# Two attention layers on one core: the first weights, the first input piece and the first theta in another order

## The chip, the cores and the metric

The kernel runs on 1 core of a Trainium2 chip. The metric is the device time of one execution in microseconds, the median of several runs. Time before: 2462.61 us (three runs, 2462.26 to 2463.37).

## What is computed

Two non-local attention blocks, one after the other, on x of 4 x 128 x 96 x 96 (float32), each with its own weights:

```python
g_x = maxpool2(conv1x1(x, g_w, g_b))          # 64 channels, 2304 keys
theta_x = conv1x1(x, theta_w, theta_b)        # 64 channels, 9216 queries
phi_x = maxpool2(conv1x1(x, phi_w, phi_b))
f = einsum('bqc,bck->bqk', theta_x, phi_x)
y = einsum('bqk,bkc->bqc', softmax(f), g_x)
W_y = conv1x1(y, W_w, W_b)
inv = bn_gamma * rsqrt(bn_var + 1e-5)
out = W_y * inv + (bn_beta - bn_mean * inv) + x
```

## The kernel before, in words

The eight blocks (four images, two layers) are worked off in one long sequence of cycles. In a cycle TensorE makes scores of 128 keys against 1024 queries (`Pair.scores`, L707), ScalarE takes their exponential (L712), VectorE adds up the denominators (L721), and TensorE multiplies by the values (`Pair.values`, L729). Keys, values and queries of the next block are made in between. All engines run their instructions in the order in which the program is written.

The change lies in the first 20 us, in which the first block is prepared:

- **Loads.** `ws[0].load_gphi` (L170, issues at L173) brings g_w by ScalarE's queue and phi_w by SyncE's. `load_x(0, 12)` (L137, issues at L135) brings the first image by SyncE in twelve pieces of 768 pixels (eight image rows, 384 KB). `load_theta` (L177) brings theta_w by ScalarE, and `columns` (L267, issues at L274) three rows of parameters (theta's bias, two variances) by ScalarE too. Every landing counts up one of eight counters that are used in turn, so a later transfer waits until the counter's last transfer has landed.
- **Warm-up.** `busy` (L993) makes TensorE multiply the identity: five times before the transpose of the weights, three times behind it (`WARM`, L58).
- **Weights.** g_w and phi_w lie in one tile; TensorE turns it (L149) and VectorE copies it to `gphiT` (L151). theta_w is turned by VectorE in eight small transposes (`steps_theta`, L160).
- **Chunks.** The product of g and phi with x is made in chunks of 512 pixels (`products`, L352), pooled by VectorE (`pool`, L336) into `stage`. Chunk 0 and 1 are eight rows by 64 pixels, chunk 2 is the sixteen rows beside them by 32 pixels, chunk 3 begins in the third piece of x. `pooled_first` (L374) makes the first four: chunk 0, the upper half of chunk 2, chunk 1, the lower half of chunk 2, chunk 3. Chunks 2 and 3 share one PSUM tile. Behind `pooled_first`, VectorE centres the keys (`centring`, L407 and L408), and pools chunks 2 and 3.
- **First theta.** The first queries (`Pair.theta`, L671) follow as soon as chunks 2 and 3 are pooled in program order, in a PSUM tile of the pool that the odd pairs of chunks use as well. ScalarE takes them with the bias (`take_theta`, L701), behind the square roots of the variances (`make_std`, L187), the load of the table for exponentials (L1029) and a batch of keys (`batch`, L413 and L419). The parameter columns that both need are turned by VectorE (`first_cols`, L160 on `square_rows`).

PSUM tiles of the two pools concerned are reused in turn: chunks 6 and 7 write the buffer of chunks 2 and 3, chunks 10 and 11 that of theta, and so wait for its readers.

Of the kernel before, what the change touches and what calls it, by code (L numbers as in the profile page):

```python
# [9 lines left out]
F32 = mybir.dt.float32  # L10
# [6 lines left out]
P = 128  # L17
# [3 lines left out]
QT = 512  # L21
# [11 lines left out]
PT = 2 * QT  # L33
# [21 lines left out]
PREPARE = (1, 4, 10)  # L55
SQ = 32
EXPS = 5
WARM = (5, 3)  # L58
CYCLE = 2 * NB
ORDER = ((0, 0), (1, 0), (0, 1), (2, 0), (1, 1), (3, 0), (2, 1), (3, 1))  # L60
SHIFT = 35.0
# [4 lines left out]
def shifted_blocks(ctx: ExitStack, tc: tile.TileContext, x: bass.AP, layers, out: bass.AP, flag):  # L66
# [24 lines left out]
    nc = tc.nc  # L91
# [9 lines left out]
    ps_sc = ctx.enter_context(tc.tile_pool(name="ps_sc", bufs=2, space=PSUM))  # L101
# [28 lines left out]
    def new_x(b):  # L130
        return xp.tile([C, HW], F32, tag="x", name=f"x_{b}")

    def load_part(b, xt, i, n):
        src = x[b].rearrange("c h w -> c (h w)")
        nc.sync.dma_start(out=xt[:, ts(i, HW // n)], in_=src[:, ts(i, HW // n)])  # L135

    def load_x(b, n=6):  # L137
        xt = new_x(b)
        for i in range(n):
            load_part(b, xt, i, n)  # L140
        return xt

    def as_row(src):
        return src.rearrange("(o c) -> o c", o=1)
# [9 lines left out]
    def turned(dst, src):  # L154

        squares = [(i, j) for i in range(src.shape[0] // SQ) for j in range(src.shape[1] // SQ)]

        def step(some):
            for i, j in some:
                nc.vector.transpose(dst[ts(j, SQ), ts(i, SQ)], src[ts(i, SQ), ts(j, SQ)])  # L160

        return [lambda n=n: step(squares[n : n + 4]) for n in range(0, len(squares), 4)]
# [104 lines left out]
    def columns(wanted, name, engine, rows=None):  # L267

        if rows is None:
            rows = prep.tile([SQ, C], F32, name=f"rows_{name}")  # L270
        nc.vector.memset(rows, 0.0)
        for i, (w, key) in enumerate(wanted):
            n = w.p[key].shape[0]
            engine.dma_start(  # L274
                out=rows[i : i + 1, :].rearrange("o (h n) -> o h n", n=n),
                in_=as_row(w.p[key]).unsqueeze(1).to_broadcast([1, C // n, n]),
            )

        def make():
            cols = const.tile([C, SQ], F32, name=f"cols_{name}")  # L280
            for step in turned(cols, rows):
                step()
            for i, (w, key) in enumerate(wanted):
                w.col[key] = cols[:, i : i + 1]

        return make
# [15 lines left out]
    class Block:  # L302
# [68 lines left out]
                for i in range(2):  # L371
                    step(j * KB + i, pss[i])

        def pooled_first(self):  # L374

            pss = self.banks(0) + self.banks(1)
            self.products(0, pss[0])
            self.products(2, pss[2], lower=False)
            self.pool(0, pss[0])
            self.products(1, pss[1])  # L380
            self.pool(1, pss[1])
            self.products(2, pss[2], upper=False)
            self.products(3, pss[3])
            return pss[2:]

# [268 lines left out]
    class Pair:  # L654
# [14 lines left out]
        def theta(self, ps):  # L669
            for h in range(2):  # L670
                nc.tensor.matmul(  # L671
                    ps[ts(h, CI), :], lhsT=self.blk.w.theta,
                    rhs=self.runs(self.blk.xt)[:, h, :], start=True, stop=True,
                )
# [269 lines left out]
    def thetas(both):  # L944
# [13 lines left out]
        return crosswise(part, take)  # L958

    ws = [Layer(l, p) for l, p in enumerate(layers)]  # L960
    ws[0].load_gphi((nc.scalar, nc.sync))
    xs = {0: load_x(0, 12)}
    ws[0].load_theta(nc.scalar)
    first_cols = columns(
        [(ws[0], "theta_b"), (ws[0], "bn_var"), (ws[1], "bn_var")], "first", nc.scalar,
        square_rows,
    )
    nc.scalar.preload_act_table(AF.Sqrt)
# [18 lines left out]
    pairs = [Pair(blk, p, n * NP + p) for n, blk in enumerate(blocks) for p in range(NP)]  # L987
# [5 lines left out]
    def busy(n):  # L993
        for i in range(n):
            nc.tensor.matmul(warm[:, :P], lhsT=ident, rhs=ident, start=True, stop=True)
# [5 lines left out]
    b0 = blocks[0]  # L1001
    busy(WARM[0])
    ws[0].make_gphi()
    for step in ws[0].steps_theta():
        step()
    busy(WARM[1])
    second_batch = b0.pooled_first()
    b0.centring(KB)
    b0.batch(0)
    for j in range(1, FIRST):  # L1010
        if j == 1:
            for i in range(KB):
                b0.pool(KB + i, second_batch[i])
            first_cols()
        else:
            b0.pooled(j)
        if j == 1:
            th = ps_sc.tile([P, PT], F32, tag="sc", name="theta_ps_0")[:, :QT]
            pairs[0].theta(th)
        if j == 3:  # L1020
            pairs[0].take_theta(th)
        if j < FIRST - 2:
            b0.batch(j)
        for i, k in {2: [(0, 0)], 3: [(0, 1)], 4: [(0, 2)], 5: [(0, 3)], 6: [(1, 0), (1, 1)]}.get(j, []):
            b0.square(i, k)
        if j == 1:
            for w in ws:
                w.make_std()
            nc.scalar.preload_act_table(AF.Exp)  # L1029
    xs[1] = load_x(1)  # L1030


# [28 lines left out]
    for n in range(1, len(blocks)):  # L1061
        first = (n - 1) * NP * NB // CYCLE * CYCLE
# [21 lines left out]
    for t in range(total + 1):  # L1084
        q, s = 2 * (t // CYCLE), t % CYCLE
        even, odd = pairs[q : q + 2] if t < total else (None, None)
        first, second, take = None, *pending
        pending = (None, None)
        if t == 1:
            first = lambda: pairs[0].values(0)  # L1090
        unit, stage_of = stages.get(t, (None, None))
        assert unit is None or (t not in keys and second is None)
        if t in keys:
            n, i = keys[t]
            first, *pending = blocks[n].chunks(i)
        elif unit:
            first, take = unit.steps[stage_of]
# [11 lines left out]
        if t < total:  # L1109
            now, j = divmod(t, NB)  # L1110
# [11 lines left out]
            if t in loads:  # L1122
                b, i = loads[t]
# [19 lines left out]
        if t:  # L1143
            before, j = divmod(t - 1, NB)
# [312 lines left out]
def nonlocal_blocks(tc: tile.TileContext, x: bass.AP, layers, out: bass.AP):  # L1457
    with tc.tile_pool(name="flag", bufs=1) as pool:
        flag = pool.tile([1, 1], I32, name="flag")
        shifted_blocks(tc, x, layers, out, flag)  # L1460
        bad = tc.nc.values_load(flag[0:1, 0:1])
        with tc.If(bad > 0):
            general_blocks(tc, x, layers, out)
# [30 lines left out]
```

## Time and profile before

| | |
|---|---|
| median of 3 runs | 2462.61 us |
| profiled execution, its own time | 2461.85 us |
| span of the profiled execution | 2460.0 us |
| granted TensorE clock, mean | 1.00 |
| TensorE matmul busy | 2452.0 us, 100% |
| VectorE busy | 2068.4 us, 84% |
| ScalarE busy | 1645.3 us, 67% |
| GpSimd busy | 755.6 us, 31% |

The span is what the profiler saw of the program; the execution's own time holds 1.85 us more. In the profile PE is TensorE's matrix product, PEld its load of weights, DVE VectorE, ACT ScalarE, POOL GpSimd and SP SyncE; ACTq and SPq are these engines' issues of DMAs. Every float32 product of 512 columns shows as two records. A row of the timeline gives start and length in us, engine, line, what is written from what, and in brackets the idle time of the engine before it and what ended that.

### The profile page before, as it was taken

To read this page: it belongs to the slowest core of one execution; us is meant where nothing else is said; L and a number is where in the kernel's file an instruction comes from. 1 tells how busy PE (TensorE), PEld (TensorE's weight loads), DVE (VectorE), ACT (ScalarE), POOL (GpSimd) and SP (SyncE) were. 2 spreads that over 40 slices of the span, in tenths; PEclk is the share of its full clock that TensorE was granted. 3 is DMA by queue.
4 is the path that set the end of the run, shared out by engine and by line. 5 is a ranking of instruction groups with operands and counts; after the bars stand their busy time and mean duration, and the time that the engine had idled before them with its cause. 6 is when DMAs were issued, how large, how long until landed. Compare 5 with 4: busy or idle time off the path is not lost.

```text
span 2460.0 us, 58074 instructions
## 1 busy us (share of the span) xinstructions
PE 2452.0 (100%) x23325; PEld 903.0 (37%) x23325; DVE 2068.4 (84%) x2652; ACT 1645.3 (67%) x1789; POOL 755.6 (31%) x850
## 2 busy tenths in 40 slices
PE   9999999999999999999999999999999999999999
PEld 3333333333333333333333333333333333333333
DVE  8988888888788888888878888888887888877777
ACT  6666666666666666666666666666666666666665
POOL 1333333332233333333223333333322333322121
PEclk9999999999999999999999999999999999999999
DMA  6566676664467666776556676666645666643443
GB/s 190 97 105 123 126 143 115 114 120 88 89 112 133 125 128 127 139 142 136 104 94 122 122 135 121 127 124 112 120 83 100 118 133 123 122 89 82 82 87 65
DMA packets 188885, 283.85 MB, mean 115 GB/s; under 512 B 33334, under 2 KB 113344, under 8 KB 188608
## 3 DMA queue, kind: packets, MB, share of 16 engines
q0 software_dynamic: 91136, 137.68, 40.1%
q1 hardware_dynamic: 97304, 142.31, 20.0%
q8 instruction: 185, 3.03, 0.5%
q14 instruction: 92, 0.75, 0.1%
q10 hardware_dynamic: 168, 0.07, 0.0%
HBM read 54.07 MB, written 35.68 MB: 36 GB/s over the span
## 4 chain that ended last, share of the span: by engine, by line
PE 100%; DMA 0%; DVE 0%; SPq 0%; issue 0%; DVEq 0%
PE av L729 45%; PE sc L707 45%; PE unit_ps L495 5%; PE W_ps L874 2%; PE gphi_ps L352 1%; PE unit_ps L504 0%; PE theta_ps L687 0%; DMA x<-in_x_dram 0%; PE gphi_ps L298 0%; PE W_ps L922 0%; PE theta_ps L298 0%; PE den_last_ps L747 0%; PE theta_ps L671 0%; DVE x L939 0%; SPq L173 0%; DVE halves L914 0%
## 5 line engine op out<-in xcount | busy, mean ns | idle before, releaser
L712 ACT ACTIVATE exp<-sc,nshift 128x1024 f32<-128x1024 f32 x1296 | 1399.3, 1113 | 758.4 <-PE sc L707 718.9
L721 DVE TENSOR_TENSOR sum<-sum,exp 128x1024 f32<-128x1024 f32 x1151 | 1407.2, 1223 | 284.3 <-ACT exp L712 231.1
L707 PE MATMUL sc<-theta,phi 64*64 64x512 f32 x10368 | 1273.9, 589 | 0.0
L729 PE MATMUL av<-exp,gT 64*64 64x512 f32 x10368 | 1229.2, 589 | 0.0
L729 PEld LDWEIGHTS av<-exp,gT 64*64 64x64 f32 x10368 | 400.0, 133 | 701.4 <-issue 681.1
L707 PEld LDWEIGHTS sc<-theta,phi 64*64 64x64 f32 x10368 | 404.3, 133 | 674.5 <-issue 628.7
L464 POOL DMA_DIRECT2D sums<-x x252 | 283.1, 1322 | 472.4 <-PE unit_ps L495 295.0
L781 POOL DMA_DIRECT2D turned<-sum x140 | 115.5, 948 | 666.3 <-DMA turned<-sum 550.1
L794 POOL DMA_DIRECT2D sum<-turned x280 | 232.7, 1221 | 113.8 <-DMA sum<-turned 102.4
L888 POOL DMA_DIRECT2D x<-halves x70 | 83.6, 1194 | 348.4 <-ACT halves L884 322.0
L495 PE MATMUL unit_ps<-sums,mixed 64*64 64x384 f32 x896 | 137.8, 482 | 0.0
L719 DVE TENSOR_TENSOR sum<-exp,exp 128x1024 f32<-128x1024 f32 x72 | 88.2, 1226 | 46.2 <-ACT exp L712 45.9
L863 POOL DMA_DIRECT2D halves<-halves x70 | 98.2, 1402 | 0.7 <-issue 0.5
L736 ACT COPY halves<-av 128x1024 f32<-128x1024 f32 x71 | 71.9, 1012 | 32.6 <-PE av L729 32.1
L614 DVE TENSOR_REDUCE pooled<-stage 128x96 f32<-128x384 f32 x168 | 91.7, 546 | 0.0
L884 ACT ACTIVATE halves<-W_ps,shift 128x512 f32<-128x512 f32 x140 | 88.6, 692 | 0.0
L874 PE MATMUL W_ps<-halves,WT 64*64 64x512 f32 x568 | 73.7, 589 | 0.0
L495 PEld LDWEIGHTS unit_ps<-sums,mixed 64*64 64x64 f32 x896 | 49.9, 133 | 61.9 <-issue 46.9
L495 PE MATMUL unit_ps<-x,mixed 64*64 64x384 f32 x448 | 68.9, 482 | 0.0
L650 DVE STREAM_TRANSPOSE gT<-pooled 32x288 f32<-32x288 f32 x112 | 52.5, 469 | 2.3
L868 DVE TENSOR_TENSOR halves<-halves 128x512 f32<-128x512 f32 x71 | 48.6, 684 | 0.0
L464 POOL DMA_DIRECT2D sums<-sums x28 | 23.1, 825 | 79.0 <-DMA sums<-x 60.2
(140 smaller groups left out, 793.9 us busy)
## 6 DMA issues: line engine op xcount, KB each, us to landing
sums<-x POOLq DMA_DIRECT2D x252, 192.0 KB, 5.5
x<-halves POOLq DMA_DIRECT2D x70, 512.0 KB, 5.3
sums<-x SPq DMA_DIRECT2D x112, 192.0 KB
turned<-sum SPq DMA_DIRECT2D x140, 128.0 KB
turned<-sum POOLq DMA_DIRECT2D x140, 128.0 KB, 3.5
halves<-halves POOLq DMA_DIRECT2D x70, 256.0 KB, 5.6
halves<-row SPq DMA_DIRECT2D x140, 128.0 KB
out_dram<-x SPq DMA_DIRECT2D x35, 512.0 KB
```

The source lines that it names most:

```text
L464: return lambda: nc.gpsimd.dma_start(out=dst(), in_=src(), accum_op=ALU.add)
L495: nc.tensor.matmul(bank[ts(c, CI), :UN], lhsT=lhsT, rhs=rhs[:, c, :], start=True, stop=True)
L614: nc.vector.tensor_reduce(pooled[:, side, ts(j, UK)].rearrange("p (h w) -> p h w", w=W // 2), self.s[:, i, :].rearrange("p (h a w b) -> p ...
L707: nc.tensor.matmul(ps[ts(c, CI), ts(h, QT)], lhsT=self.blk.keys_of(k, c, h), rhs=self.th[ts(h, CI), :], start=True, stop=True,)
L712: nc.scalar.activation(e, ps, AF.Exp, bias=nshift)
L721: nc.vector.tensor_add(self.sum, self.sum, e)
L729: nc.tensor.matmul(self.av[ts(h, CI), ts(r, QT)], lhsT=self.blk.gT[ts(r, CI), k, :], rhs=e[ts(r, CI), ts(h, QT)], start=(k == 0), stop=(k ...
L781: nc.gpsimd.dma_start(out=self.turned[ts(h, CI)], in_=self.sum[ts(h, CI), ts(h, QT)], accum_op=ALU.add,)
L794: nc.gpsimd.dma_start(out=folded()[ts(i, SQ)], in_=self.turned[ts(i, SQ), ts(k, n)], accum_op=ALU.add,)
L863: nc.gpsimd.dma_start(out=self.y, in_=self.halves[:, QT:], accum_op=ALU.add)
L874: nc.tensor.matmul(self.pss[h][ts(c, CI), :], lhsT=self.blk.w.W[ts(h, CI), ts(c, CI)], rhs=self.y[ts(h, CI), :], start=True, stop=True,)
L884: nc.scalar.activation(self.halves[:, ts(h, QT)], self.pss[h], AF.Identity, bias=self.blk.w.shift,)
```

## The change

ScalarE issues g_w, phi_w and theta_w, in this order. SyncE issues x alone, and its first piece as two halves of four image rows each. Chunk 0 is made in two halves accordingly. The three parameter rows are issued by GpSimd. The first theta is made between the lower half of chunk 2 and chunk 3. There are two warm-up products behind the transpose in place of three. `load_first` is called with an empty function for `between`.

```diff
-WARM = (5, 3)
+WARM = (5, 2)
...
+    def load_first(b, n, between):
+        xt = new_x(b)
+        load_part(b, xt, 0, 2 * n)
+        between()
+        load_part(b, xt, 1, 2 * n)
+        for i in range(1, n):
+            load_part(b, xt, i, n)
+        return xt
...
-        def pooled_first(self):
+        def pooled_first(self, theta):
             pss = self.banks(0) + self.banks(1)
-            self.products(0, pss[0])
+            self.products(0, pss[0], lower=False)
+            self.products(0, pss[0], upper=False)
             self.products(2, pss[2], lower=False)
             self.pool(0, pss[0])
             self.products(1, pss[1])
             self.pool(1, pss[1])
             self.products(2, pss[2], upper=False)
+            theta()
             self.products(3, pss[3])
             return pss[2:]
...
-    ws[0].load_gphi((nc.scalar, nc.sync))
-    xs = {0: load_x(0, 12)}
+    ws[0].load_gphi((nc.scalar, nc.scalar))
     ws[0].load_theta(nc.scalar)
+    xs = {0: load_first(0, 12, lambda: None)}
     first_cols = columns(
-        [...], "first", nc.scalar, square_rows,
+        [...], "first", nc.gpsimd, square_rows,
     )
...
-    second_batch = b0.pooled_first()
+    th = []
+    def first_theta():
+        th.append(ps_sc.tile([P, PT], F32, tag="sc", name="theta_ps_0")[:, :QT])
+        pairs[0].theta(th[0])
+    second_batch = b0.pooled_first(first_theta)
...
-        if j == 1:
-            th = ps_sc.tile([P, PT], F32, tag="sc", name="theta_ps_0")[:, :QT]
-            pairs[0].theta(th)
         if j == 3:
-            pairs[0].take_theta(th)
+            pairs[0].take_theta(th[0])
```

More of the change, by code (lines that the diff above doesn't have):

```diff
@@ L960, in shifted_blocks @@
     ws = [Layer(l, p) for l, p in enumerate(layers)]
-    ws[0].load_gphi((nc.scalar, nc.sync))
-    xs = {0: load_x(0, 12)}
+    ws[0].load_gphi((nc.scalar, nc.scalar))
     ws[0].load_theta(nc.scalar)
+    xs = {0: load_first(0, 12, lambda: None)}
     first_cols = columns(
-        [(ws[0], "theta_b"), (ws[0], "bn_var"), (ws[1], "bn_var")], "first", nc.scalar,
+        [(ws[0], "theta_b"), (ws[0], "bn_var"), (ws[1], "bn_var")], "first", nc.gpsimd,
         square_rows,
```

## The prediction, made before the change was run

> **What bounds the kernel now.** I read the page first (busy time by engine), then the table of stretches for TensorE, then the chain that ended last, and last the timeline of the first 20 us, where every edit lies. From the page:
>
> ```profile
> span 2460.0 us, 58074 instructions
> PE 2452.0 (100%) x23325; PEld 903.0 (37%) x23325; DVE 2068.4 (84%) x2652; ACT 1645.3 (67%) x1789; POOL 755.6 (31%) x850
> ```
>
> From the table of stretches, TensorE alone (length, busy time, records, granted clock, DMA share, GB/s):
>
> ```profile
> 0.00:5.60 5.60, 3.56 (x18) 1.00 0.58 166
> 5.60:20.00 14.40, 14.40 (x76) 1.00 0.75 273
> 20.00:2440.00 2420.00, 2420.00 (x23088) 1.00 0.61 114
> ```
>
> TensorE never idles between 5.60 and 2440 us at a granted clock of 1.00. So the span is the time up to the first real product, plus a fixed amount of TensorE work, plus whatever stalls the change opens. The chain at its start (start, us, what):
>
> ```profile
> 1.38 4.09 DMA x<-in_x_dram
> 5.46 0.14 issue
> 5.60 3.71 PE gphi_ps L352 x20
> 9.30 0.86 PE theta_ps L671 x4
> 10.16 8.65 PE gphi_ps L352 x40
> 18.82 1.02 PE sc L707 x8
> ```
>
> The chain goes back through the first product, at 5.60, to the first piece of x. One chunk (four records) is 0.86 us: ten take 8.65. Four chunks, theta and ten chunks are 15 steps, 12.9 us at 0.86, and the rows give 3.71 + 0.86 + 8.65 = 13.2: before hides all but 0.3 us of stalls. So there are two levers, the 5.60 us and new stalls. The timeline has what feeds them (start, us, engine line, [idle before it <- what ended that]):
>
> ```profile
> 0.73 0.59 SPq L173 DMA_DIRECT2D gphi_nat<-in_L_conv_phi_w_dram  x1
> 0.74 0.61 ACTq L173 DMA_DIRECT2D gphi_nat<-in_L_conv_g_w_dram  x1
> 1.38 8.67 SPq L135 DMA_DIRECT2D x<-in_x_dram  x12
> 1.38 0.85 ACTq L177 DMA_DIRECT2D theta_nat<-in_L_conv_theta_w_dram  x1
> 3.44 0.23 PEld L149 LDWEIGHTS gphiT_ps<-ident,gphi_nat 128*128 128x128 f32 x1
> 3.65 0.42 PE L149 MATMUL gphiT_ps<-ident,gphi_nat 128*128 128x128 f32 x1
> 4.11 0.29 DVE L151 COPY gphiT<-gphiT_ps 128x128 f32<-128x128 f32 x1 [2.64 <-PE gphiT_ps L149]
> 5.69 1.71 DVE L160 STREAM_TRANSPOSE thetaT<-theta_nat 32x32 f32<-32x32 f32 x8 [1.29 <-DMA theta_nat<-in_L_conv_theta_w_dram]
> 8.23 1.08 PE L352 MATMUL gphi_ps<-x,gphiT 128*64 128x512 f32 x4
> 9.21 0.15 DVE L408 TENSOR_SCALAR centre<-centre 64x1 f32<-64x1 f32 x1
> 9.39 1.29 DVE L336 TENSOR_REDUCE stage<-gphi_ps 128x128 f32<-128x512 f32 x2
> 10.71 0.85 DVE L160 STREAM_TRANSPOSE cols_first<-square_rows 32x32 f32<-32x32 f32 x4
> 11.59 1.29 DVE L336 TENSOR_REDUCE stage<-gphi_ps 128x128 f32<-128x512 f32 x2
> 11.66 0.48 ACT L187 ACTIVATE std<-cols_first,eps 128x1 f32<-128x1 f32 x2
> 12.16 1.28 ACT L1029 ACT_TABLE_LOAD   x1
> 13.46 0.50 ACT L413 ACTIVATE phi<-stage,centre 64x256 f32<-64x256 f32 x1
> 13.99 0.40 ACT L419 COPY phi<-phi 64x256 f32<-64x256 f32 x1
> 14.42 0.69 ACT L701 ACTIVATE theta<-theta_ps,cols_first 128x512 f32<-128x512 f32 x1
> 15.16 0.20 PEld L352 LDWEIGHTS gphi_ps<-x,gphiT 128*64 128x64 f32 x4 [0.73 <-ACT theta L701]
> ```
>
> The last row is the one to see. The eleventh chunk writes the PSUM buffer that theta occupied, and starts at 15.16, right behind ScalarE's copy of theta (14.42 + 0.69 = 15.11). Behind that copy there is no slack: std, the table load, a batch of keys and the copy follow each other on ScalarE from 11.66, and std waits for VectorE's parameter columns (10.71 + 0.85 = 11.56), which follow the pools of the third and fourth chunk (9.39). Whatever moves those pools moves TensorE at 15.16.
>
> **The change part by part.** First, the weights. phi_w was SyncE's first issue, and is now ScalarE's second, the place that theta_w had (issue at 1.38). In that place theta_w landed at 5.69 (VectorE's wait ends there), 4.31 us after its issue, because the first x piece was issued at the same moment and moved on the same 16 DMA engines. First in their queues, g_w and phi_w were there by 3.44 (TensorE's weight load of both), 2.70 after 0.74. So phi_w lands between 1.38 + 2.70 = 4.08 and 5.69. The x ahead of it now starts 0.65 earlier (0.73 in place of 1.38), and the two halves hold the bytes of one piece: 5.69 - 0.65 = 5.04 is my estimate, and it is nearest the theta_w row, since the place in the queues is the same. By the Trainium skill, DMA: Bandwidth & Descriptors (Anatomy of one DMA), a transfer is some 2.0 us plus its bytes over 436 GB/s; an estimate by it puts phi_w at 1.38 + 2.1 = 3.5 and the start before 5 us. The theta_w row, 4.31 for the same 32 KB, is against it, so the sum goes by the row.
>
> From both weights to the end of VectorE's copy was 3.44 to 4.40, 0.96 us; with 0.15 for the step to a product (the 0.14 of "issue" in the chain) the first product starts at 5.04 + 0.96 + 0.15 = 6.15 or so, 0.6 later than 5.60. Ends: 5.2 to 6.8, so -0.4 to +1.2. The first half of x is no longer the bound: the whole piece took 4.09, and 0.73 + 4.09 = 4.82. Halving costs TensorE nothing (the columns are the same, and the program has such halves already, in its third chunk); its gain is hidden behind the weights. One warm-up matmul less shortens the queue behind the transpose, which is idle time anyway.
>
> Second, theta's step. On TensorE, before (lines of before.py; DMAHW and DVE are the landings and the engine waited for):
>
> ```order
> L352 MATMUL gphi_ps_0_0_1_174<-x_113,gphiT_159 64x512 [waits DMAHW6_49]
> L352 MATMUL gphi_ps_0_0_1_174<-x_113,gphiT_159 64x512
> L352 MATMUL gphi_ps_0_1_175<-x_113,gphiT_159 64x256 x2
> L352 MATMUL gphi_ps_0_1_175<-x_113,gphiT_159 64x512 [waits DMAHW0_49]
> L352 MATMUL gphi_ps_0_1_175<-x_113,gphiT_159 64x512
> L671 MATMUL theta_ps_199<-x_113,thetaT_161 64x512 [waits DVE_49]
> L671 MATMUL theta_ps_199<-x_113,thetaT_161 64x512
> ```
>
> and now, at the same place:
>
> ```order
> L361 MATMUL gphi_ps_0_0_1_174<-x_115,gphiT_160 64x512 [waits DMAHW5_49]
> L361 MATMUL gphi_ps_0_0_1_174<-x_115,gphiT_160 64x512
> L361 MATMUL gphi_ps_0_1_175<-x_115,gphiT_160 64x256 x2
> L682 MATMUL theta_ps_188<-x_115,thetaT_162 64x512 [waits DVE_49]
> L682 MATMUL theta_ps_188<-x_115,thetaT_162 64x512
> L361 MATMUL gphi_ps_0_1_175<-x_115,gphiT_160 64x512 [waits DMAHW6_49]
> L361 MATMUL gphi_ps_0_1_175<-x_115,gphiT_160 64x512
> ```
>
> Theta's two rows went ahead of the fourth chunk's. It spares the wait for the third piece of x, which is at most the 0.3 us above. But the third and fourth chunk share one PSUM tile, and VectorE's pools of both wait for its last write: the fourth chunk ended at 8.23 + 1.08 = 9.31 and the pools began at 9.39, with the centring just done (9.21 + 0.15 = 9.36). With theta ahead the fourth chunk ends 0.86 later, less some 0.06 of the spared wait: the pools slip by 0.8 against TensorE's start.
>
> The wait on theta_w stands at VectorE's head too: behind it queue every pool, and behind those ScalarE's batches. theta_w is ScalarE's third issue, after one piece of x more. At 6.15 (0.45 later than 5.69) its transposes, two pools and the centring end at 9.36 + 0.45 = 9.8. The fourth chunk ends at 9.31 + 0.55 + 0.80 = 10.7, so it is the later, by 0.9, and theta_w is covered; without that cover it would cost one for one.
>
> Sum: pools of chunks three and four at 9.39 + 1.35; columns, std, table load, batch and theta's copy as long as before, so the copy ends at 15.11 + 1.35 = 16.5. TensorE, 0.55 late, would be at the eleventh chunk at 15.7 and waits 0.8. **From there on it is 1.4 us late**; later waits (exp, value products) hang on the same engines, which moved by as much.
>
> Third, the parameter rows. On ScalarE, before:
>
> ```order
> L173 DMA gphi_nat_110<-in_L_conv_g_w_dram 64x128
> L177 DMA theta_nat_126<-in_L_conv_theta_w_dram 64x128
> L274 DMA square_rows<-in_L_conv_theta_b_dram 1x2x64 [waits DVE_49]
> L274 DMA square_rows<-in_L_conv_bn_var_dram 1x128 x2
> L968 ACT_TABLE_LOAD
> ```
>
> and now:
>
> ```order
> L182 DMA gphi_nat_110<-in_L_conv_g_w_dram 64x128
> L182 DMA gphi_nat_110<-in_L_conv_phi_w_dram 64x128
> L186 DMA theta_nat_113<-in_L_conv_theta_w_dram 64x128
> L979 ACT_TABLE_LOAD
> ```
>
> The three rows left ScalarE's queue for GpSimd's, behind its identity mask. The nearest rows for their cost, and ScalarE's first work after its table load (the last row but one gives GpSimd's first transfers, the last the size and the median us to landing of that line's 252):
>
> ```profile
> 1.01 0.29 POOL masks.py:199 TENSOR_SCALAR_AFFINE_SELECT ident<-ident 128x128 f32<-128x128 f32 x1
> 9.39 0.50 ACT L413 ACTIVATE phi<-stage,centre 64x256 f32<-64x256 f32 x1 [4.08 <-DVE centre L408]
> 38.52 2.13 POOL L464 DMA_DIRECT2D sums<-x  x2 [37.22 <-DMA sums<-x]
> sums<-x POOLq DMA_DIRECT2D x252, 192.0 KB, 5.5
> ```
>
> GpSimd has nothing between 1.3 and 38 us, and ScalarE idles 4.08 us for VectorE's centring before 9.39, so the issues are free. Three issues at 1.07 from 1.3 end at 4.5, and 5.5 to landing makes 10.0, before the columns at 10.71 + 1.35 = 12.1. The cover is 2 us; beyond it a late row costs one for one. SyncE issues twelve pieces in thirteen transfers, none behind a weight, and its later ones wait for earlier landings as before.
>
> On the profiled execution (span 2460.0, 2461.85 with the 1.85 around it) the sum gives 2463.2; the median of the runs is 0.76 above it (2462.61), so 2464.0.
>
> **The rivals.** *The weights aren't queued behind x.* If the engines take phi_w ahead of the second half, it lands near 4.4, the product starts at 5.5, and only theta's 0.8 is left, less 0.1: +0.7, 2463.3. At the lower end (4.08) it is +0.4. The fit cited above would have it so, or earlier. For it: the halves are shorter than the piece that theta_w met; against: its 4.31. By the Trainium skill, the same page (Queues, rings and completion order), an engine takes turns between queues packet by packet, which leaves both halves ahead of phi_w if the first half comes first; the 4.31 agrees.
>
> *A cold TensorE, the slower side.* The warm-up runs in two rates (timeline, the first ten records and two windows):
>
> ```profile
> 1.35 2.50 PE L995 MATMUL warm_ps<-ident 128*128 128x128 f32 x10 [1.35 <-POOL ident masks.py:199]
> 1.94 1.49 PE L995 MATMUL warm_ps<-ident 128*128 128x128 f32 x6
> 4.08 0.84 PE L995 MATMUL warm_ps<-ident 128*128 128x128 f32 x5
> ```
>
> Six records took 1.49, the five from 4.08 on 0.84: the rate doubles some 3 us after TensorE's first matmul at 1.35. Now it goes idle after the first five warm-up matmuls (3.65) until phi_w lands. If the doubling has to begin again at 5.0 and comes at 8.1, the products from 6.15 to 8.1 run at half rate and lose 0.95: +2.3, 2465.0. To exceed 0.2% (4.9 us) it would need 7 us at half rate. By the Trainium skill, TensorE: Matmul & The Clock Gate (Part 1), full rate takes about 3.4 us of sustained work in a window that runs freely; the rows agree with the length, none shows a gap inside it.
>
> *It gains.* Weights at the lower end, and theta's copy no bound because ScalarE finds slack I don't see: the start's -0.4 stays, 2462.2. Against it is the zero slack at 15.16.
>
> *Rows late on GpSimd's queue.* A landing at 14 costs 2 us more, 2466.
>
> **How the numbers follow.** Forecast +1.4: 0.50; weights early 0.22; cold TensorE 0.16; gain 0.08; rows late 0.04. The time is that of the likeliest, 2464.0. The range runs from the gain's end (2462.2, less likely than the weights' +0.4) to just past the cold case: 2462.3 to 2465.6. A measurement of this kernel tells 0.2% or 4.9 us from no change; no case reaches it on the fast side (5.6 us is all that lies ahead of the first product), and only a longer cold stretch or rows 4 us late on the slow side: faster 0.01, same 0.97, slower 0.02.
>
> **What would show it.** Right: TensorE's weight load of both weights near 5.0, the first product near 6.15, pools of chunks three and four near 10.7, and TensorE waiting 0.8 us for theta's copy near 16.5. Wrong: the first product before 5.6, chunks of over 0.86 us at the start, VectorE waiting for the parameter rows, or no wait for theta's copy.

## The result and the profile after

The changed kernel took 2465.82 us, median of 22 runs (2464.50 to 2466.76), beside 2462.25 us of the kernel before on the same chip (22 runs, 2461.56 to 2463.75): ratio 1.0014, 95% interval 1.0008 to 1.002. It is 3.6 us slower, 0.14%, within the 0.2% that the prediction counted as no change. It lies above the forecast of 2464.0 us and above its range, 2462.3 to 2465.6 us.

TensorE alone, in the same three stretches as before (length, busy time, records, granted clock, DMA share, GB/s):

```profile
0.00:5.60 5.60, 2.50 (x10) 1.00 0.61 187
5.60:20.00 14.40, 13.96 (x65) 1.00 0.73 269
20.00:2440.00 2420.00, 2420.00 (x23078) 1.00 0.61 114
```

Behind 20 us TensorE is busy without a gap, as before. Ahead of it there are fewer records in the first two stretches (75 for 94), although the program has not become shorter (23327 records in all for 23325): what was done by 20 us is now done later. The chain says where:

```profile
1.31 4.15 DMA gphi_nat<-in_L_conv_phi_w_dram
5.47 0.14 issue
5.60 0.45 PE gphiT_ps L158
6.05 0.85 PE warm_ps L1006 x4
6.90 4.19 PE gphi_ps L361 x20
11.09 0.86 PE theta_ps L682 x4
11.95 6.04 PE gphi_ps L361 x28
17.98 0.41 issue
18.40 3.65 PE gphi_ps L361 x16
22.05 1.02 PE sc L718 x8
```

The first product was at 5.60 and is at 6.90; the first score was at 18.82 and is at 22.05, 3.23 us later. From there to the end the chain of before and that of after have the same length but for some tenths in the last transfer: of the 3.5 us between the spans (2460.0 and 2463.5), 3.23 lie ahead of the first score.

Three rows of the chain are new. It now begins with phi_w, which takes 4.15 us. The twenty records of the first three chunks take 4.19 us. And there is a piece of "issue" at 17.98, in which TensorE stands ahead of the eleventh chunk. The timeline of the changed kernel has what lies around them:

```profile
1.36 2.50 PE L1006 MATMUL warm_ps<-ident 128*128 128x128 f32 x10 [1.36 <-POOL ident masks.py:199]
5.60 0.45 PE L158 MATMUL gphiT_ps<-ident,gphi_nat 128*128 128x128 f32 x1 [1.73 <-DMA gphi_nat<-in_L_conv_phi_w_dram]
6.09 0.29 DVE L160 COPY gphiT<-gphiT_ps 128x128 f32<-128x128 f32 x1 [4.61 <-PE gphiT_ps L158]
6.83 4.26 PE L361 MATMUL gphi_ps<-x,gphiT 128*64 128x256 f32 x20
12.86 1.29 DVE L345 TENSOR_REDUCE stage<-gphi_ps 128x128 f32<-128x512 f32 x2 [0.82 <-PE gphi_ps L361]
14.17 0.85 DVE L169 STREAM_TRANSPOSE cols_first<-square_rows 32x32 f32<-32x32 f32 x4
15.06 1.29 DVE L345 TENSOR_REDUCE stage<-gphi_ps 128x128 f32<-128x512 f32 x2
16.38 0.75 DVE L441 STREAM_TRANSPOSE gT<-stage 32x192 f32<-32x192 f32 x2
17.06 1.24 DVE L345 TENSOR_REDUCE stage<-gphi_ps 128x128 f32<-128x512 f32 x2
17.88 0.69 ACT L712 ACTIVATE theta<-theta_ps,cols_first 128x512 f32<-128x512 f32 x1
18.37 0.23 PEld L361 LDWEIGHTS gphi_ps<-x,gphiT 128*64 128x64 f32 x4 [1.29 <-PE gphi_ps L361]
18.40 3.65 PE L361 MATMUL gphi_ps<-x,gphiT 128*64 128x512 f32 x16 [0.44 <-PE gphi_ps L361]
```

Two things to see. TensorE's first warm-up ends at 3.86, and the next work, the transpose of the weights, begins at 5.60, when phi_w has come: 1.73 us idle in between. And the eleventh chunk loads its weights at 18.37 and starts at 18.40, while ScalarE's copy of theta runs until 17.88 + 0.69 = 18.57. It did not wait for that copy. What ended just ahead of it are VectorE's pools of chunks 6 and 7, 17.06 + 1.24 = 18.30.

### The profile page after: what moved, and what is told of

It is laid out like the page before. It is cut to its first block, busy times and chain, and to the rows that moved or that the text cites. A ratio compares the mean times of both kernels' runs of the same rounds, so it can differ in the third digit from the quotient of the medians.

```text
span 2463.5 us, 58080 instructions
## 1 busy us (share of the span) xinstructions
PE 2453.7 (100%) x23327; PEld 903.8 (37%) x23327; DVE 2067.6 (84%) x2652; ACT 1646.4 (67%) x1789; POOL 755.7 (31%) x853
## 4 chain that ended last, share of the span: by engine, by line
PE 99%; DMA 0%; DVE 0%; issue 0%; ACTq 0%; DVEq 0%
PE av L740 45%; PE sc L718 45%; PE unit_ps L506 5%; PE W_ps L885 2%; PE gphi_ps L361 1%; PE unit_ps L515 0%; PE theta_ps L698 0%; DMA gphi_nat<-in_L_conv_phi_w_dram 0%; PE gphi_ps L307 0%; PE W_ps L933 0%; PE theta_ps L307 0%; PE den_last_ps L758 0%; PE theta_ps L682 0%; PE warm_ps L1006 0%; DVE x L950 0%
```

## The experiments

The first theory: three pieces on one chain, namely phi_w's late landing, a TensorE that falls back to half rate in the idle time behind its warm-up, and theta ahead of the fourth chunk, paid for at the eleventh. The rivals: the third queue (GpSimd's rows) or the halves hold phi_w up; half rate is covered by VectorE and the loads; theta's place is free.

Each kernel was timed 11 times beside 27 to 33 runs of the kernel before on the same chip. The interval of each of these ratios reaches 0.0008 to 0.001 to either side, some 2 us, and the kernel before against itself came out at +0.39 us. By its interval alone a kernel is told from before only where it is 2.6 us or more later (e2, e4 to e7, e14, e17). What is smaller rests on medians of 11 and on the traces, and under 0.5 us on the traces alone; each trace is one execution. In the table the two starts are from the timeline of each profiled execution, and "between" is the one less the other.

| kernel | first product | first score | between | median, us | over before |
|---|---|---|---|---|---|
| before | 5.60 | 18.75 | 13.15 | 2462.25 | |
| changed | 6.83 | 21.98 | 15.15 | 2465.82 | +3.57 |
| e1 changed, phi_w on SyncE first | 4.86 | 19.60 | 14.74 | 2463.02 | +0.78 |
| e2 changed, theta back | 6.86 | 21.97 | 15.11 | 2465.18 | +2.94 |
| e3 changed, 12 warm-ups | 7.46 | 21.16 | 13.70 | 2464.35 | +2.11 |
| e4 changed, rows on ScalarE | 6.69 | 21.98 | 15.29 | 2465.09 | +2.85 |
| e5 changed, again | 6.87 | 22.09 | 15.22 | 2465.39 | +3.27 |
| e6 rows on ScalarE, again | 6.66 | 22.73 | 16.07 | 2465.32 | +3.20 |
| e7 changed, first piece whole | 7.08 | 22.16 | 15.08 | 2465.93 | +3.81 |
| e8 before, theta ahead | 5.13 | 18.82 | 13.69 | 2462.16 | +0.04 |
| e9 before, again | 5.34 | 19.22 | 13.88 | 2462.50 | +0.39 |
| e10 before, theta ahead, again | 5.28 | 19.02 | 13.74 | 2462.38 | +0.27 |
| e11 before, halves | 4.85 | 19.09 | 14.24 | 2462.21 | +0.10 |
| e12 before, almost no warm-up | 5.31 | 20.68 | 15.37 | 2463.75 | +1.64 |
| e13 before, theta ahead, columns late | 5.35 | 19.01 | 13.66 | 2462.26 | -0.14 |
| e14 changed, columns late | 6.67 | 22.40 | 15.73 | 2465.19 | +2.79 |
| e15 before, halves, theta, columns late | 4.85 | 19.32 | 14.47 | 2462.63 | +0.23 |
| e16 before, theta ahead, keys late | 5.94 | 18.97 | 13.03 | 2462.29 | +0.07 |
| e17 changed, keys late | 7.09 | 21.83 | 14.74 | 2464.85 | +2.63 |
| e18 before, halves, theta, keys late | 4.85 | 18.80 | 13.95 | 2462.06 | -0.16 |

**e1, phi_w back on SyncE ahead of x.**

```diff
-    ws[0].load_gphi((nc.scalar, nc.scalar))
+    ws[0].load_gphi((nc.scalar, nc.sync))
```

> The changed kernel with phi_w back on SyncE, ahead of x; halves, theta's place and GpSimd's rows stay. First theory (three pieces on one chain: the late phi_w, a TensorE that fell back to half rate in the idle time behind its warm-up, and theta ahead of the fourth chunk): phi_w lands near 3 us again, the first product starts at 4.7 to 5.6 us at full rate, so both the 1.2 us of the start and the 1.3 to 1.4 us of half rate go and theta's 0.86 us is what is left: 2462.3 to 2463.3 us. Rival (GpSimd's rows, a third queue that starts at 1.65 us, hold the transfers up): weights and x land late here too, and the time stays at 2464.5 us or more.

Measured 2463.02, +0.78 over before and within the expectation. Its timeline:

```profile
3.66 0.42 PE L158 MATMUL gphiT_ps<-ident,gphi_nat 128*128 128x128 f32 x1
4.86 1.95 PE L361 MATMUL gphi_ps<-x,gphiT 128*64 128x256 f32 x12
7.21 1.51 PE L361 MATMUL gphi_ps<-x,gphiT 128*64 128x512 f32 x8 [0.40 <-DMA x<-in_x_dram]
```

Everything else of the change is in this kernel, GpSimd's rows too, and the weights' transpose is back at 3.66. So it is phi_w's place behind g_w on ScalarE that makes the late start, and no third queue. What the start gains against the kernel before (4.86 for 5.60) goes again in two places. The first twelve records, of 256 columns, would take 1.29 us at the rate of 0.86 for four of 512, and take 1.95: in part they run at half rate, which the expectation had ruled out. And at 7.21 TensorE waits for x's third transfer. The wait at the eleventh chunk is in this profile too (0.41 of "issue" in its chain).

**e2, theta back behind the fourth chunk.**

```diff
             self.products(2, pss[2], upper=False)
-            theta()
             self.products(3, pss[3])
+            theta()
```

> The changed kernel with theta's products behind the fourth chunk instead of ahead of it; all loads as changed. First theory: the pools of chunks 2 and 3 come 0.86 us earlier and nothing behind them has slack, so 0.86 us goes: about 2464.9 us, and the eleventh chunk at 17.5 instead of 18.4 us. Rival (theta's place is free, since VectorE has waited out the half rate by then and the loss is made elsewhere): unchanged, 2465.5 to 2466.1 us.

Measured 2465.18, between the two. Its chain, and from its timeline the load of the eleventh chunk's weights:

```profile
6.93 5.55 PE gphi_ps L361 x24
12.48 0.86 PE theta_ps L682 x4
13.34 8.70 PE gphi_ps L361 x40
18.38 0.20 PEld L361 LDWEIGHTS gphi_ps<-x,gphiT 128*64 128x64 f32 x4 [0.78 <-ACT theta L712]
```

The forty records behind theta run without a piece of waiting, so the wait at the eleventh chunk is gone. Its weights are loaded right behind ScalarE's copy of theta (17.64 + 0.69 = 18.33), as in the kernel before, and TensorE is not yet out of work. But the first score of this profile is where it was (21.97), because half rate lasted longer: 24 records are four chunks, and 5.55 less 0.86 for the fourth leaves 4.69 for the three that took 4.19 in the changed kernel. The wait's price and the length of half rate cannot be parted by one profile of each.

**e3, a warm-up that lasts until phi_w has landed.**

```diff
-WARM = (5, 2)
+WARM = (12, 2)
```

> The changed kernel with 12 warm-up transposes instead of 5 ahead of the weights' transpose, so that TensorE is busy until phi_w lands; nothing else is changed. First theory: the first products start at 6.8 to 7.0 us as before this edit, but 0.21 us apart instead of 0.42, and the 1.3 to 1.4 us of half rate goes, less 0.1 to 0.2 us if the longer warm-up ends behind phi_w: 2464.3 to 2464.7 us. Rival (the half rate costs nothing at the end, because theta_w's landing at 6.27 us and VectorE's transposes and pools behind it set the pace): 2465.5 to 2466.1 us, with products at full rate and longer waits of TensorE for pools.

Measured 2464.35, within the expectation, 1.0 to 1.5 us below the changed kernel. Its chain:

```profile
1.36 5.49 PE warm_ps L1006 x24
6.85 0.21 PE gphiT_ps L158
7.06 0.47 PE warm_ps L1006 x4
7.53 2.74 PE gphi_ps L361 x20
```

The same twenty records take 2.74 us, where they took 4.19, although they start 0.6 later. **That is the half rate, 1.45 us in this pair**, and the rival that it is covered falls. Even with TensorE busy from 1.36 on, the rate doubled only near 6.9: four records behind the transpose took 0.47, and 0.85 in the changed kernel. The changed kernel's warm-up, ten records in 2.50, was thus at half rate throughout: TensorE did not fall back from a rate that it had reached, it had not reached it when the idle time began.

**e4, e5 and e6, the rows back on ScalarE, the changed kernel again, and the rows once more.**

```diff
-        [...], "first", nc.gpsimd, square_rows,
+        [...], "first", nc.scalar, square_rows,
```

> The changed kernel with the three parameter rows back on ScalarE's queue, behind the weights. First theory: the rows are off the chain and do not hold phi_w up: 2465.5 to 2466.1 us, phi_w landing at 5.3 to 5.6 us as with GpSimd's rows. Rival (the third queue delays phi_w on the shared DMA engines): phi_w lands 0.5 us or more earlier, near the 5.04 us that was forecast, and the time falls by as much, to 2465.3 us or less.

> The changed kernel itself once more, as the yardstick for the other runs on the same chip, since the runs with theta put back and with the rows on ScalarE came out 0.6 to 0.7 us below its first median. First theory (the moment at which TensorE's rate doubles isn't tied to the program, so executions differ by up to 2 us): single times again spread over about 2 us, 2464.5 to 2466.8 us, with a median of 2465.5 to 2466.1 us. Rival (the 0.6 to 0.7 us were a difference of chips or hours, and those two edits did nothing): a median near 2465.1 us.

> The rows on ScalarE's queue once more, beside the changed kernel on the same chip. If the rows on GpSimd's queue hold phi_w up, as the first run of this edit would have it by its time, it is 0.5 to 0.8 us below the changed kernel here too, with phi_w's landing 0.15 us or more earlier. If they are off the chain, the two agree within 0.3 us.

The first run gave 2465.09, 0.7 below the changed kernel's median, which is the rival's number. On one chip with the changed kernel (2465.39) the same edit gave 2465.32. So the 0.7 was not the edit's, and the changed kernel itself, 0.4 lower here, came out between its two expectations: some 0.4 of the difference was of chip or hour. The first products moved 0.14 and 0.21 us ahead, as phi_w landed that much earlier. The rows on GpSimd's queue cost no more than that. Single times spread over 1.7 to 2.4 us in these three runs, but over 2.2 and 2.4 in the kernel before beside them, so the spread alone does not show the half rate. That its length differs by execution is in the profiles; the profiled execution of e6, the slowest of its eleven, has the twenty records at the slow end:

```profile
6.73 5.10 PE gphi_ps L361 x20
```

**e7, x's first piece whole.**

```diff
-    xs = {0: load_first(0, 12, lambda: None)}
+    xs = {0: load_x(0, 12)}
```

> The changed kernel with x's first piece in one transfer instead of two. First theory: x is on time either way, near 4 us against phi_w's 5.5 us, and phi_w waits for the same bytes ahead of it: within 0.3 us of the changed kernel. Rival (phi_w is held up by the second half's own packets in the queues): phi_w lands up to 0.4 us earlier, and the time falls by as much or, with the shorter idle time, somewhat more.

Measured 2465.93, not told from the changed kernel. phi_w landed later, not earlier (chain):

```profile
1.32 4.39 DMA gphi_nat<-in_L_conv_phi_w_dram
7.15 4.12 PE gphi_ps L361 x20
```

The rival falls. The second row is the fast end of the seven profiles that have these twenty records behind the idle time: 4.12 to 5.10, mean 4.47. Against 2.74 half rate costs 1.4 to 2.4 us, 1.7 in the mean.

**e8, e9 and e10, theta ahead in the kernel before, and the kernel before itself.**

```diff
             self.products(2, pss[2], upper=False)
+            theta()
             self.products(3, pss[3])
```

> The kernel before with one edit: theta's products ahead of the fourth chunk, with the loads of before. First theory: TensorE starts at 5.60 us at full rate, the pools of chunks 2 and 3 slip by 0.8 us and the eleventh chunk waits 0.6 us for VectorE's pools: first score 0.6 to 0.85 us later, 2462.9 to 2463.1 us. Rival (theta's place is free where nothing else is late): 2462.0 to 2462.5 us.

> The kernel before itself, for a second profile and for what two equal kernels differ by. The sum that the traces so far bear out: the first score stands 13.15 us behind the first product plus what half rate and the wait at the eleventh chunk cost, and everything behind the first score is the same in all kernels. So here: no wait at the eleventh chunk, first score 13.1 to 13.2 us behind the first product, which may stand anywhere from 5.0 to 5.7 us as x lands at 4.8 to 5.5 us; median within 0.3 us of the kernel before. Rival (a wait at the eleventh chunk comes and goes by execution): over 13.4 us between the two.

> The kernel before with theta's products ahead of the fourth chunk, once more, since its first median was no later than that of the kernel before although its trace showed a wait of 0.61 us at the eleventh chunk. First theory (the wait is there in every execution, and the earlier median was luck in x's landing): 13.7 us from the first product to the first score, and a median 0.4 to 0.7 us above the kernel before. Rival (something in other executions of the kernel before costs as much, such as first products at half rate, so that theta's place is free): median within 0.25 us of it again.

Here the first theory's price falls: +0.04 and +0.27, beside +0.39 for the kernel before itself (at most 0.3 had been expected for the latter, and 0.4 to 0.7 for e10 by the first theory). Yet the wait is there. The chain of e8:

```profile
5.20 2.73 PE gphi_ps L352 x16
7.93 0.86 PE theta_ps L672 x4
8.79 6.03 PE gphi_ps L352 x28
14.82 0.42 issue
15.24 3.65 PE gphi_ps L352 x16
```

The timeline of the second profile of the kernel before shows what it stands against:

```profile
5.34 2.80 PE L352 MATMUL gphi_ps<-x,gphiT 128*64 128x512 f32 x16 [0.39 <-DMA x<-in_x_dram]
8.74 1.08 PE L352 MATMUL gphi_ps<-x,gphiT 128*64 128x512 f32 x4 [0.60 <-DMA x<-in_x_dram]
```

In this execution the fourth chunk waited 0.60 us for x's third piece; in the first profile TensorE ran through. So without theta ahead it is 13.15 or 13.88 us from the first product to the first score, by the landing, and with theta ahead 13.69 and 13.74: theta fills the wait for x, and the eleventh chunk pays for it. The expectation of e9 had the larger number as a rival, but put the wait at the eleventh chunk; it is at the fourth. How often the third piece is late, two profiles do not say.

**e11, the halves alone on the kernel before** (`load_first`, two products of chunk 0, `WARM = (5, 2)`).

> The kernel before with the halves alone: x's first piece in two transfers and two products of the first chunk, one warm-up less; the weights, theta and the rows as before. First theory: x's first half lands 0.5 us or more earlier than the whole piece, the first product starts at 4.8 to 5.0 us, right behind the warm-up, in part at half rate, and TensorE then waits for x's second piece or not, without a wait at the eleventh chunk: 2461.5 to 2462.2 us, the first of all versions that could beat the kernel before. Rival (x's later pieces set the pace): the wait for them grows by what the start gains, within 0.2 us of the kernel before.

Measured 2462.21, the rival's number, not told from before. The first product moved to 4.85, as expected, and the first score did not move forward: the first twelve records take 2.22 us (timeline) where 1.29 would be full rate, and then TensorE waits for x (chain):

```profile
2.47 4.74 DMA x<-in_x_dram
7.21 0.04 issue
7.25 2.37 PE gphi_ps L361 x12
```

**e12, the kernel before almost without its warm-up.**

```diff
-WARM = (5, 3)
+WARM = (1, 0)
```

> The kernel before with one warm-up transpose ahead of the weights' transpose instead of five and none behind it; all loads and products as before. First theory: the first product stays at 5.0 to 5.6 us, but TensorE's rate doubles only 3 to 5.5 us behind it, so 1.3 to 2.3 us go at half rate: 2463.5 to 2464.7 us, with single times spread over 1.5 us or more. Rival (half rate in the first chunks is covered by VectorE and the loads): within 0.4 us of the kernel before.

Measured 2463.75, +1.64, within the expectation. None of the change's edits is in it. The first product is at 5.31, and the first four chunks, 3.71 us in the kernel before, take (chain):

```profile
5.31 5.97 PE gphi_ps L352 x20
```

So some 2.26 us of half rate can be made in the kernel before by leaving TensorE idle ahead of its first product, and they reach the end: in its profile the first score is 1.93 later than before, with a start that is 0.29 earlier.

**e13, e14 and e15, the parameter columns one step later**: on the kernel before with theta ahead, on the changed kernel, and on the kernel before with halves and theta.

```diff
-            first_cols()
...
+        if j == 2:
+            first_cols()
...
-        if j == 1:
+        if j == 2:
             for w in ws:
                 w.make_std()
```

> The kernel before with theta's products ahead of the fourth chunk, and the parameter columns (with std and the table load behind them) one step later, behind VectorE's pools of chunks 4 and 5. First theory (the wait at the eleventh chunk is for VectorE's pools of chunks 6 and 7, which stand behind the columns): the wait of 0.61 us is gone, 13.1 us from the first product to the first score, and the time falls by 0.3 to 0.6 us against the kernel before: 2461.5 to 2461.9 us. Rival (theta ahead was free because nothing waits there in most executions): no later or earlier than the kernel before, 2462.0 to 2462.4 us, though the trace shows no wait.

> The changed kernel with the parameter columns one step later, behind VectorE's pools of chunks 4 and 5. First theory: the wait of 0.61 us at the eleventh chunk goes and nothing else, about 2465.0 to 2465.2 us against 2465.4 to 2465.8 us of the changed kernel. Rival (theta's copy, now later on ScalarE, holds up the first score): unchanged or slower, with a wait ahead of the first score.

> The kernel before with what should gain: the halves, theta ahead of the fourth chunk and the columns one step later; weights and rows on their queues of before. First theory: the first product at 4.85 us, some 0.5 us of half rate or of waits for x's second piece, no wait for the third and none at the eleventh chunk: 2461.3 to 2461.8 us. Rival (x's pieces give back whatever is gained in front of them): 2462.0 us or more.

Measured 2462.26, 2465.19 and 2462.63. That the time of e14 is the expected one is luck, and the other two came out at their rivals' times. By the trace all three missed, with the wait still there, 0.26 to 0.29 us in place of some 0.4 (chain of e13):

```profile
15.16 0.26 issue
15.43 3.65 PE gphi_ps L352 x16
```

The edit was aimed badly: one step later the columns still stand ahead of the pools of chunks 6 and 7, so VectorE's work in front of these was nearly the same.

**e16, e17 and e18, the first transposes of keys behind the pools of chunks 6 and 7**, on the same three kernels, the columns in their old place.

```diff
-{2: [(0, 0)], 3: [(0, 1)],
+{3: [(0, 0), (0, 1)],
```

> The kernel before with theta's products ahead of the fourth chunk, and VectorE's first transposes of keys (0.74 us) behind its pools of chunks 6 and 7 instead of ahead of them. First theory (the wait at the eleventh chunk is for those pools): they end 0.75 us earlier and 0.2 us ahead of the eleventh chunk, the wait of 0.61 us is gone, 13.1 us from the first product to the first score, and the median falls below the kernel before by what theta's cover of x's third piece is worth, 0.2 to 0.5 us: 2461.6 to 2462.0 us. Rival (the wait is for something else): it stays at 0.4 us or more, 2462.1 to 2462.5 us.

> The changed kernel with the same edit, the first transposes of keys behind the pools of chunks 6 and 7. First theory: the wait of 0.61 us goes and nothing takes its place: 2464.8 to 2465.2 us, against 2465.4 to 2465.8 us of the changed kernel and 2465.2 us with theta put back. Rival (another wait takes its place ahead of the first score): 2465.4 us or more.

> The kernel before with the halves, theta ahead of the fourth chunk and the first transposes of keys behind the pools of chunks 6 and 7; weights and rows on their queues of before. First theory: as the run with the columns late, whose first score stood at 19.32 us in its profile, less its wait of 0.5 us: 2461.8 to 2462.2 us, no gain over the kernel before that could be told, since what the earlier start brings goes at half rate and for x's second piece. Rival: the pieces add up, 2461.6 us or less.

Now the wait is gone in all three. The chain of e17:

```profile
11.60 0.86 PE theta_ps L682 x4
12.46 9.44 PE gphi_ps L361 x44
21.90 1.02 PE sc L718 x8
```

and VectorE, with ScalarE's copy of theta, in its timeline:

```profile
15.57 2.52 DVE L345 TENSOR_REDUCE stage<-gphi_ps 128x128 f32<-128x512 f32 x4
18.01 1.50 DVE L441 STREAM_TRANSPOSE gT<-stage 32x192 f32<-32x192 f32 x4
18.40 0.69 ACT L712 ACTIVATE theta<-theta_ps,cols_first 128x512 f32<-128x512 f32 x1
```

The pools of chunks 4 to 7 end at 18.09, and the chain of TensorE has no piece of waiting. The eleventh chunk, six chunks and the fourth behind theta, begins near 18.5 (12.46 and seven times 0.86), while theta is still being copied, until 19.09. That settles which buffer it was: not theta's. The price: in the changed kernel the same 44 records took 6.04 + 0.41 + 3.65 = 10.10, here 9.44, so 0.66 us (0.61 counted between the starts of neighbouring products, as the expectations have it). The median of e17 is 0.5 to 1.0 below the changed kernel's two, as expected, which the interval does not tell and the trace does; that of e16 (2462.29) is its rival's number and not below the kernel before, so what the cover of x's third piece is worth there stays untold. In its profile x's first piece landed late and the first product stood at 5.94. e18 is the fastest by its median, 2462.06, and not told from the kernel before: no version was found that beats it.

## Why the prediction was wrong, point by point

- **What bounds the kernel**: right. TensorE has no idle time behind the first score, in any of these kernels, and all that changed lies ahead of it.
- **phi_w's landing**: the direction was right and the size off. It landed at 5.47, not 5.04; 4.15 us behind its issue, close to theta_w's 4.31 in that place in the kernel before. The 0.65 by which x's issue was moved ahead did not carry over. In e7, with the whole piece ahead, it was 4.39. By the Trainium skill, DMA: Bandwidth & Descriptors (Anatomy of one DMA), an estimate is some 2.1 us, from a fit that the section gives for GpSimd's transfers; phi_w, on ScalarE's queue, took 4.15. From the turns that the queues take packet by packet the prediction concluded that both halves stay ahead of phi_w. That does not follow, since turns would let phi_w in between; its landing was late all the same, and no view here shows the order of the packets.
- **From both weights to the first product**: 0.96 + 0.15 was forecast, and it was 1.43 by the chain of the changed kernel (5.47 to 6.90). The prediction called the warm-up behind the transpose idle time. In the chain it is on the path: 0.85 us at half rate between the transpose and the first product, while VectorE's copy was done at 6.09 + 0.29 = 6.38. That it cost about 0.3 us follows from these rows; a kernel without it wasn't tried.
- **A cold TensorE**: this is the step that failed. The forecast put it at nothing, as a rival with a chance of 0.16 and a price of 0.95. It came in all eight late kernels that kept the short warm-up, at 1.45 us in the first profile and 1.4 to 2.4 in others, and e3 and e12 show it from both sides. The price was too low because the rate does not double a fixed 3.1 us after work resumes. From the twenty records the half rate lasted twice the loss: 2 x 1.45 = 2.9 us from 6.90, to 9.8, 4.2 us behind the transpose at 5.60; in e6 2 x 2.36 = 4.7 from 6.73, to 11.4. By the Trainium skill, TensorE: Matmul & The Clock Gate (Part 1), the window runs freely, and the doubling depends on where in it the first product falls. The traces agree that it varies, but more widely than the 0.5 us to either side that the Trainium skill gives there: some 3.0 us behind the first record in the kernel before, 5.5 in e3.
- **Theta ahead of the fourth chunk**: the wait at the eleventh chunk was forecast at 0.8 and is 0.66, but the mechanism failed. The prediction carried the row of before over to the new order. With theta behind the fourth chunk (before, e2, e9, e11, e12) the eleventh chunk's weights are loaded 0.05 behind theta's copy, as that row has it. With theta ahead, TensorE waits for VectorE's pools of chunks 6 and 7 (18.30 and 18.37 in the changed kernel) and not for the copy, so the eleventh chunk then writes another buffer than theta's. Why the order of the products changes the buffer, no run shows; that buffers are handed out in turn does not hold for both orders. And "at most the 0.3 us" that it would spare at x's third piece was too little: 0.60 in one of two profiles of the kernel before, which would make theta's place free there, as the times of e8 and e10 have it. In the changed kernel everything starts so late that x has long landed, there is nothing to spare, and the wait is paid.
- **Halves and rows**: free as far as the times tell, as forecast (e7; e6 beside e5). In the traces the rows on GpSimd's queue make phi_w 0.14 to 0.21 us later.
- **The signs of being wrong**: two of those that it named came, chunks of over 0.86 us at the start (twenty records, three chunks, in 4.19) and no wait for theta's copy.

The sum of the two profiles, by their chains: start +1.30, half rate +1.45, wait at the eleventh chunk +0.66, less 0.12 (before took 13.22 from product to score, e16, without any waits, 13.10): 3.29, against 3.23 measured. The forecast had +1.4 in place of it; half rate is the largest part of what it lacked, and the start, 1.30 for 0.55, most of the rest.

## What to carry to other kernels

A warm-up is worth what it does for the first real product: if TensorE goes idle between the two because a weight comes late (here 1.6 to 2.0 us, behind 2.5 us of warm-up), the first products run at half rate, and then a late load costs its own delay and half rate on top. So price a load that is moved back together with the idle time that it opens on TensorE. And before a step is moved to fill a wait, look at more than one execution for that wait, and at which buffer the next user of its PSUM pool gets in the new order.

## What the runs showed of the hardware that was not expected

- The granted clock of the profile reads 1.00 in the stretch 5.60 to 20.00 of the changed kernel, in which its first products run at half rate. Here only the length of a known group of records shows it (4.19 against 2.74).
- TensorE can be busy without a gap for over 5 us before its rate doubles (e3: from 1.36 to some 6.9), or some 3.0 (before: 1.35 to some 4.4).
- A shorter idle time did no such harm: in e16 the warm-up's six records behind the transpose still ran at half rate (1.43 us, 1.05 in the kernel before), TensorE then idled 0.65 us, and the sixteen records from 5.94 on took 2.80, the full rate.
- phi_w, 32 KB and the second of ScalarE's queue, took 3.9 to 4.4 us in the eight late kernels with the short warm-up, with 384 KB of x issued ahead of it in one transfer (4.39) or in two (3.94 to 4.41). As the first of a queue it was there within 2.7 us.
